# Linear attention in a vision tower: q formed with features on partitions, its row norm applied at the residual

## The chip, the cores and the metric

The kernel runs on one core of one Trainium2 chip, in fp32 throughout. The metric is the device time of one execution in microseconds (us), as the median of several runs. One further execution was taken by the hardware profiler, and all views of the profile come from that one.

## The reference

A small vision tower: a tokenizer, then two layers. Layer 0 is an attention over the four images and a mixture of six experts (top 2). Layer 1 is a linear attention and a smaller mixture of four experts with a shared branch. There are 4 images of 784 tokens of 256 features. The tokenizer puts the same tokens three times in a row, so the kernel computes one copy and writes it three times. The change concerns the linear attention of layer 1:

```python
qkv = x @ W_qkv + b_qkv                       # x: layernorm(h)
q, k, v = jnp.split(qkv, 3, axis=2)
q = q - jnp.mean(q, axis=2, keepdims=True)
k = k - jnp.mean(k, axis=2, keepdims=True)
q2, k2 = q * q, k * k
k2 = l2_normalize(k2 / (sum(k2, axis=2) + 1e-7), axis=-2)    # over the tokens
q2 = l2_normalize(q2 / (sum(q2, axis=2) + 1e-7), axis=-1)    # over the features
kv = jnp.einsum('bnc,bnd->bcd', k2, v)
attn = v + jnp.einsum('bnc,bcd->bnd', q2, kv) / math.sqrt(N)
h = h + attn @ W_out + b_out
```

Dividing q2 by its row sum and then by its row's length leaves a row divided by its length alone, apart from the small constants.

## The kernel before

The work is a sequence of stages on one core. From about 314 us on, layer 0's experts run in blocks of 256 rows. The rows of a block are loaded, transposed, taken through three matrices and written back to DRAM. For each block, `own_weights` (L1145) copies the expert's weights on DVE, `turned` (L1152) transposes on PE and copies on ACT, `hidden` (L1165) computes the two hidden layers (tile `pb`, evicted half by ACT and half by DVE into `hb`), and `rows_back` (L1184) the output (tile `pyb`, evicted by DVE into `yb`). In the loop over the later blocks (L1437) the order on DVE and SP is written out by hand: the program fixes it. The other engines' orders come from a scheduler.

In that loop, at its second block, stands the call of `centred_weights()` (L577, called at L1447). It takes the mean over the 256 output features out of the q and k weights (L580 to L582) and out of their bias (L587 to L589), all on DVE. After that, q and k come out of the matmul already centred. The bias `bqkv` lies on 112 partitions, the same row on each.

The linear attention works on *units*: each image of seven tiles of 112 tokens is cut into a unit of four tiles and one of three, eight units in all. What happens to a unit:

- `fetch` (L1360): gathers of the expert outputs, two for each tile, issued by POOL one after another. The gathers of units 0 to 2 are issued from the block loop, those of unit 2 once the last block has been written.
- `stats_one` (L1377) and `normalise` (L1395): DVE adds the gathered rows to the residual h (L1383), takes mean and variance, and makes the normalised rows `xa` (L1406).
- `x_t` (L1419): PE transposes them (helper, L297), ACT and DVE each copy one half out (L81, L83), into `lxT`.
- `q_k` (L1558): for each tile, two matmuls of 512 columns give q and k with tokens on partitions (L1574). DVE adds the bias (L1578), ACT squares each half in place and sums it along the row (L1582), and squares q2 again for the sum of its fourth powers (L1583).
- `scales` (L1591): the row factors, from those sums; ACT scales k (L1606), DVE scales q (L1607), ACT squares the scaled k (L1611). `fold` (L1614) adds these squares over the tiles on DVE (L1618 to L1623).
- `q_t` (L1625): PE transposes the scaled q (L297), ACT and DVE copy it out into `lqT`.
- `k_x` (L1630), for one image: the column norms of k2 (L1635), and the product of k2 with the normalised rows (tile `pukx`, L1648). `g_t` (L1657) and `kv_out` (L1668) make of it `kvo`, the 256 by 256 matrix that a row of q2 is multiplied with.
- `rows_out` (L1682): for two tiles at a time, one PSUM bank collects the product of `lxT` with `Wvo` (L1689) and of `lqT` with `kvo` (L1694); DVE adds it to h (L1700).

`layer1_weights` (L593) makes `Wvo`, the product of the v weights with the output weights, in unit 1's turn: PE transposes the v weights (L598), DVE copies them out as `WvT` (L602), and PE multiplies (L607).

The order around the change is set by the loop over units (from L1704), which calls these functions in a staggered way: the rows of unit u-2 are put out while unit u is begun. The scheduler moves instructions on PE, ACT and DVE from there. PSUM tiles named by `ps_tile` come from a pool of seven banks; the eighth bank, `psum_s`, serves small results in turn, among them the column norms of k2 and the gate of the last expert layer.

After the linear attention, seven groups of four tiles go through layer 1's experts (from about 666 us). They start once the h of their rows is complete.

Of the kernel before, what the change touches and what calls it, by code (L numbers as in the profile page):

```python
# [21 lines left out]
F32 = mybir.dt.float32  # L22
I32 = mybir.dt.int32
AF = mybir.ActivationFunctionType
# [3 lines left out]
P = 128  # L28
TT = 112
# [31 lines left out]
def tile_vit_tower(ctx: ExitStack, tc: tile.TileContext, a: dict, out: bass.AP):  # L61
# [10 lines left out]
    def ps_tile(name):  # L72
        return psum.tile([P, 512], F32, tag="ps", name=name)
# [251 lines left out]
    def halves(tiles):  # L325
        return [tiles[i : i + 2] for i in range(0, len(tiles), 2)]
# [3 lines left out]
    def cut(t0, n):  # L330
        return slice(t0 * TT, (t0 + n) * TT)
# [245 lines left out]
    def centred_weights():  # L577
        qkw = Wqkv[:, :, : 2 * D].rearrange("p c (i d) -> p c i d", i=2)
        mean = w1p.tile([P, 2, 2], F32, tag="mean", name="mean")
        nc.vector.tensor_reduce(mean, qkw, AX.X, ALU.add)  # L580
        nc.vector.tensor_scalar(mean, mean, 1.0 / D, None, ALU.mult)
        nc.vector.tensor_tensor(  # L582
            qkw, qkw, mean.unsqueeze(3).to_broadcast([P, 2, 2, D]), ALU.subtract
        )
        qkb = bqkv[:, : 2 * D].rearrange("p (i d) -> p i d", i=2)
        meanb = w1p.tile([TT, 2], F32, tag="meanb", name="meanb")
        nc.vector.tensor_reduce(meanb, qkb, AX.X, ALU.add)  # L587
        nc.vector.tensor_scalar(meanb, meanb, 1.0 / D, None, ALU.mult)
        nc.vector.tensor_tensor(  # L589
            qkb, qkb, meanb.unsqueeze(2).to_broadcast([TT, 2, D]), ALU.subtract  # L590
        )

    def layer1_weights():  # L593
        WvT = w1p.tile([P, 2, D], F32, tag="WvT", name="WvT")
# [742 lines left out]
    bqkv = spread(w1p, "bqkv", a["L1_attn_b_qkv"], nc.sync)  # L1337
    bout = spread(w1p, "bout", a["L1_attn_b_out"], nc.sync)

# [37 lines left out]
    def stats_one(u, j):  # L1377
        if u >= len(units) or j >= units[u][2]:
            return
        b, j0, n = units[u]  # L1380
        t = b * TPI + j0 + j
        for k in range(2):
            nc.vector.scalar_tensor_tensor(  # L1383
                h[:, t, :], ys[u][:, j, k, :], wk[:, k, t : t + 1], h[:, t, :],
                ALU.mult, ALU.add,
            )
# [166 lines left out]
    late = [early]  # L1553

    lin = linear.enter_context(tc.tile_pool(name="lin", bufs=2, reuse_waits="tile"))
    sumsof = {}

    def q_k(u, j0, j1):  # L1558

        n = units[u][2]  # L1560
        xT = xTs[u]
        if j0 == 0:
            qks[u] = lin.tile([TT, GT, 2 * D], F32, tag="qk", name="qk")
            sumsof[u] = (
                small.tile([TT, GT, 2], F32, tag="ss", name="ss"),
                small.tile([TT, GT], F32, tag="s4", name="s4"),
            )
        qk = qks[u]
        ss, s4 = sumsof[u]
        junk = lin.tile([TT, D], F32, tag="junk", name="junk", bufs=1)  # L1570
        for j in range(j0, min(j1, n)):
            pqk = ps_tile("pqk")[:TT]
            for c in range(2):
                nc.tensor.matmul(  # L1574
                    pqk, xT[:, c, cut(j, 1)], Wqkv[:, c, : 2 * D],
                    start=(c == 0), stop=(c == 1),
                )
            nc.vector.tensor_tensor(qk[:, j, :], pqk, bqkv[:, : 2 * D], ALU.add)  # L1578

            for i in range(2):  # L1580
                half = qk[:, j, i * D : (i + 1) * D]
                nc.scalar.activation(half, half, AF.Square, accum_out=ss[:, j, i : i + 1])  # L1582
            nc.scalar.activation(junk, qk[:, j, :D], AF.Square, accum_out=s4[:, j : j + 1])  # L1583
            if u:
                stats_one(u + 1, j)
        if j1 >= n and u:
            if u + 1 < len(units) and units[u + 1][2] > n:
                stats_one(u + 1, n)
            normalise(u + 1)

    def scales(u):  # L1591

        b, j0, n = units[u]
        qk = qks[u]
        ss, s4 = sumsof.pop(u)

        nc.vector.tensor_scalar(ss[:, :n], ss[:, :n], 1e-7, None, ALU.add)
        nc.scalar.activation(s4[:, :n], s4[:, :n], AF.Sqrt, bias=zero[:TT])
        nc.vector.scalar_tensor_tensor(
            ss[:, :n, 0], ss[:, :n, 0], 1e-12, s4[:, :n], ALU.mult, ALU.max  # L1600
        )
        nc.vector.reciprocal(ss[:, :n], ss[:, :n])
        uk = uks[u] = lin.tile([TT, GT, D], F32, tag="uk", name="uk", bufs=3)
        sq = lin.tile([TT, GT, D], F32, tag="sq", name="sq", bufs=1)
        for j in range(n):
            nc.scalar.activation(uk[:, j, :], qk[:, j, D:], AF.Copy, scale=ss[:, j, 1:2])  # L1606
            nc.vector.tensor_scalar(  # L1607
                qk[:, j, :D], qk[:, j, :D], ss[:, j, 0:1], None, ALU.mult
            )
        for j in range(n):  # L1610
            nc.scalar.activation(sq[:, j, :], uk[:, j, :], AF.Square)  # L1611
        return sq

    def fold(u, sq):  # L1614
# [4 lines left out]
        else:  # L1619
# [1 line left out]
            nc.vector.tensor_tensor(acc, acc, sq[:, 0:2, :], ALU.add)  # L1621
            nc.vector.tensor_tensor(acc[:, 0, :], acc[:, 0, :], sq[:, 2, :], ALU.add)
            nc.vector.tensor_tensor(acc[:, 0, :], acc[:, 0, :], acc[:, 1, :], ALU.add)  # L1623

    def q_t(u):  # L1625
        n = units[u][2]
        qT = qTs[u] = lin.tile([P, 2, GN], F32, tag="lqT", name="lqT", bufs=3)
        transposed(qks.pop(u), n, lambda c, pt: copy_out(qT[:, c, : n * TT], pt))

    def k_x(b):  # L1630

# [49 lines left out]

    def rows_out(u):  # L1682
        b, j0, n = units[u]
        xT, qT, kvo = xTs.pop(u), qTs.pop(u), kvos[b]
        for two in halves(range(n)):
            pm = ps_tile("pout")[:TT].rearrange("p (t d) -> p t d", t=2)
            for i, j in enumerate(two):
                for c in range(2):
                    nc.tensor.matmul(  # L1689
                        pm[:, i, :], xT[:, c, cut(j, 1)], Wvo[:, c, :],  # L1690
                        start=(c == 0), stop=False,
                    )
                for c in range(2):
                    nc.tensor.matmul(  # L1694
                        pm[:, i, :], qT[:, c, cut(j, 1)], kvo[:, c, :],
                        start=False, stop=(c == 1),
                    )
            t = b * TPI + j0 + two[0]
            ht = h[:, t : t + len(two), :]
            nc.vector.tensor_tensor(ht, pm[:, : len(two), :], ht, ALU.add)  # L1700

# [3 lines left out]
    for u in range(len(units) + 2):  # L1705
        b, odd = divmod(u - 2, 2)
        one_image = u >= 2 and not odd
        if u == 0:
            fetch(3)
            x_t(1)  # L1710
            q_k(0, 0, GT)
            squares[0] = scales(0)
            fold(0, squares.pop(0))
            continue
        if u < len(units):
            fetch(u + 3)
        if u == len(units):
            shared = shared1(0)
        if one_image:
            k_x(b)  # L1720
            q_t(u - 1)
        if u == 2:
            gT = g_t(0)
            kv_out(0, gT)
            rows_out(0)
            x_t(2)
        if u < len(units):
            q_k(u, 0, 2)
        if one_image and b:
            gT = g_t(b)  # L1730
        if u < len(units):
            q_k(u, 2, GT)
            if u == 1:
                lw.extend(layer1_weights())
                Wvo, bvo = lw[:2]
            squares[u] = scales(u)
        if one_image and b:
            kv_out(b, gT)
        if u == len(units) - 1:
            rows_in(0)  # L1740
            turn_rows(0)
            gate(0)
        if 2 <= u < len(units) - 1:
            x_t(u + 1)
        if u == 3:
            for k in range(3):
                residual(k)
        if u >= 2 and (b or odd):
            rows_out(u - 2)
        if u < len(units):  # L1750
            fold(u, squares.pop(u))
            if u % 2:
                q_t(u - 1)
    linear.close()

    with tc.tile_pool(name="ffn1", bufs=2) as work:
# [92 lines left out]
```

## Time and profile before

| what | us |
|---|---|
| median of 3 runs (852.16 to 854.61) | 854.3 |
| profiled execution, its own time | 813.35 |
| its span, first to last instruction | 811.6 |
| PE (TensorE matmul) busy | 735.7 |
| DVE (VectorE) busy | 514.5 |
| ACT (ScalarE) busy | 318.5 |
| block loop, the later blocks | to about 503 |
| linear attention | about 504 to 666 |
| last expert layer | about 666 to 812 |

The engines are PE, with PEld for its weight loads, DVE, ACT, POOL (GpSimd) and SP (SyncE). A line of the timeline gives the start, the duration, the engine and the line of the program, the tiles written and read, the number of instructions merged into the line, and, in brackets, the idle time before it with what ended it. An fp32 matmul leaves two records, so "x8" on PE are four matmuls. A line of the table of stages gives the stretch, its length, the busy time of each engine with its number of instructions, the granted PE clock (1.00 is full speed), the share of the DMA engines and the rate in GB/s.

### The profile page before, as it was taken

How to read it: one execution, taken by the hardware profiler on the slowest of the kernel's cores; microseconds unless marked ns; L12 is line 12 of the kernel's file. 1: busy time of each engine (PE TensorE's matmuls, PEld its weight loads, DVE VectorE, ACT ScalarE, POOL GpSimd, SP SyncE). 2: the span in 40 equal slices, each digit the busy share in tenths (PEclk: the TensorE clock that was granted, in tenths of full speed). 3: DMA queues.
4: the chain of work that ended last, by engine and by line, in shares of the span. 5: the costliest groups of instructions: out<-in, count | busy, mean ns of one | idle time of the engine just before them, and what ended most of it. 6: DMA issues, size and time to landing. Idle time of an engine off the chain costs nothing. (4 is left out here: it accounts for less than half of the span.)

```text
span 811.6 us, 11184 instructions
## 1 busy us (share of the span) xinstructions
PE 735.7 (91%) x3669; PEld 519.4 (64%) x3669; DVE 514.5 (63%) x1619; ACT 318.5 (39%) x758; POOL 132.5 (16%) x151
## 2 busy tenths in 40 slices
PE   1879998899798887999999999799999999999996
PEld 1757785555455555887888887375776675555553
DVE  3477887576668886436445756699985655554431
ACT  0414443545375475443222322627544503222221
POOL 4200000000006360760012030775000000000000
PEclk9999999999999988999999999899999999999999
DMA  8999992000001168443334234232000002333323
GB/s 182 343 426 422 420 421 85 1 0 1 0 1 56 36 207 260 137 139 104 94 101 137 92 107 131 85 86 69 1 1 1 0 20 69 88 98 93 94 85 113
DMA packets 59182, 97.52 MB, mean 120 GB/s; under 512 B 15486, under 2 KB 49460, under 8 KB 54260
## 3 DMA queue, kind: packets, MB, share of 16 engines
q1 hardware_dynamic: 52700, 81.47, 29.1%
q0 software_dynamic: 6224, 14.13, 6.1%
q10 hardware_dynamic: 200, 1.21, 0.7%
q8 instruction: 29, 0.48, 0.2%
q14 instruction: 29, 0.24, 0.1%
HBM read 31.04 MB, written 65.74 MB: 119 GB/s over the span
## 5 line engine op out<-in xcount | busy, mean ns | idle before, releaser
L901 POOL DMA_INDIRECT xrows<-xn,pos x56 | 60.2, 1074 | 274.2 <-ACT kq L665 233.4
L1369 POOL DMA_INDIRECT ys<-yrows,pos x56 | 57.0, 1018 | 142.1 <-DMA yrows<-yb 126.0
L1173 PE MATMUL pb<-xTb,own 128*128 128x256 f32 x240 | 58.8, 389 | 3.8 <-DVE r L764 1.6
L1173 PE MATMUL pb<-hb,own 128*128 128x256 f32 x240 | 57.1, 380 | 0.3 <-DVE hb L1181 0.3
L1190 PE MATMUL pyb<-own,hb 128*128 128x256 f32 x240 | 57.0, 380 | 0.2 <-ACT hb L1179 0.2
L1179 ACT ACTIVATE hb<-pb,own 128x256 f32<-128x256 f32 x74 | 35.0, 473 | 55.9 <-PE pb L1173 47.5
L297 PE MATMUL pt<-ident,xn 112*128 112x112 f32 x280 | 42.2, 282 | 12.6 <-DVE xn L482 6.9
L1173 PEld LDWEIGHTS pb<-xTb,own 128*128 128x128 f32 x240 | 44.6, 194 | 12.5 <-ACT hb L1179 1.9
L1574 PE MATMUL pqk<-Wqkv,lxT 128*112 128x512 f32 x112 | 49.7, 594 | 0.5 <-ACT lxT L81 0.5
L1190 PEld LDWEIGHTS pyb<-own,hb 128*128 128x128 f32 x240 | 45.4, 190 | 6.7 <-ACT hb L1179 0.6
L297 PEld LDWEIGHTS pt<-ident,xn 112*128 112x128 f32 x280 | 32.4, 148 | 26.6 <-ACT xn L778 9.6
L1173 PEld LDWEIGHTS pb<-hb,own 128*128 128x128 f32 x240 | 43.3, 190 | 5.9 <-DVE hb L1181 0.9
L1196 DVE TENSOR_TENSOR yb<-pyb,eb 128x512 f32<-128x512 f32 x30 | 20.7, 690 | 39.2 <-PE pyb L1190 38.8
L306 PE MATMUL pe<-xT,eW 128*128 128x448 f32 x112 | 45.2, 546 | 0.0
L1163 ACT COPY xTb<-ptb 128x512 f32<-128x512 f32 x30 | 17.5, 583 | 64.3 <-PE ptb L1159 64.3
L1181 DVE TENSOR_SCALAR hb<-pb,own 128x256 f32<-128x256 f32 x46 | 22.1, 481 | 29.5 <-PE pb L1173 29.5
L317 PE MATMUL pwo<-Wo,oT 128*112 128x256 f32 x112 | 29.0, 413 | 7.5 <-DVE oT L730 6.7
L1574 PEld LDWEIGHTS pqk<-Wqkv,lxT 128*112 128x112 f32 x112 | 19.3, 177 | 24.8 <-issue 22.7
L690 DVE SCALAR_TENSOR_TENSOR prod<-kq 128x784 f32<-128x784 f32 x32 | 30.3, 968 | 7.3 <-ACT kq L665 5.1
L1582 ACT ACTIVATE qk<-qk 112x256 f32<-112x256 f32 x56 | 22.8, 407 | 27.9 <-DVE qk L1578 25.4
L306 PEld LDWEIGHTS pe<-xT,eW 128*128 128x128 f32 x112 | 20.2, 190 | 20.9 <-issue 20.7
L1150 DVE COPY own<-ew 128x1540 f32 x30 | 28.9, 963 | 5.0 <-issue 1.5
(339 smaller groups left out, 1520.1 us busy)
## 6 DMA issues: line engine op xcount, KB each, us to landing
xrows<-nothing SPq DMA_DIRECT2D x19, 1024.0 KB
yrows<-nothing SPq DMA_DIRECT2D x19, 1024.0 KB
out_dram<-h SPq DMA_DIRECT2D x84, 112.0 KB
xb<-xrows SPq DMA_DIRECT2D x30, 256.0 KB
yrows<-yb SPq DMA_DIRECT2D x30, 256.0 KB
ew<-in_L_ffn_expert_w_dram SPq DMA_DIRECT2D x6, 768.0 KB
wb<-wd SPq DMA_DIRECT2D x28, 112.0 KB
img<-in_x_dram ACTq DMA_DIRECT2D x2, 588.0 KB
```

Source lines behind the costliest of these rows:

```text
L297: nc.tensor.transpose(pt[:, j * TT : (j + 1) * TT], xn[:, j, c * P : (c + 1) * P], ident[:TT, :TT])
L306: nc.tensor.matmul(pm[: wcols.stop - wcols.start, :n], w[:, c, wcols], xT(c), start=(c == 0), stop=(c == chunks - 1),)
L317: nc.tensor.matmul(pm[:, i, :], xT(c, t), w[:, c, :], start=(c == 0), stop=(c == chunks - 1))
L690: nc.vector.scalar_tensor_tensor(prod, qTs[s][:, o, :], 1.0, kT[:, o, t * SEQ : (t + 1) * SEQ], ALU.mult, ALU.mult, accum_out=atts[s][:, o ...
L901: put = nc.gpsimd.indirect_dma_start(out=xrows[:, :], out_offset=bass.IndirectOffsetOnAxis(ap=pos[:, k, t0 + j : t0 + j + 1], axis=0), in_ ...
L1150: nc.vector.tensor_copy(w, ewf[0][:, bass.ds(off, EW)])
L1173: nc.tensor.matmul(pm, wm[:, c, o * P : (o + 1) * P], src[:, c, :], start=(c == 0), stop=(c == 1),)
L1179: nc.scalar.activation(dst[:, o, :], pm, AF.Relu, bias=b)
L1190: nc.tensor.matmul(pm[:, t, :], src[:, c, t * P : (t + 1) * P], wm[:, c, :], start=(c == 0), stop=(c == 1),)
L1369: got = nc.gpsimd.indirect_dma_start(out=y[:, j, k, :], out_offset=None, in_=yrows[:, :], in_offset=bass.IndirectOffsetOnAxis(ap=pos[:, k, ...
L1574: nc.tensor.matmul(pqk, xT[:, c, cut(j, 1)], Wqkv[:, c, : 2 * D], start=(c == 0), stop=(c == 1),)
L1582: nc.scalar.activation(half, half, AF.Square, accum_out=ss[:, j, i : i + 1])
```

## The change

q and k are formed apart. k is formed as before, with tokens on partitions, but two tiles share a PSUM bank and one bias addition. q is formed transposed, with the weights as the stationary operand: features on partitions, up to 448 tokens in one matmul. ACT squares it at eviction and adds the bias as a column. That column, `bq`, is made in `centred_weights`, by two matmuls with a single one that turn the bias row. The transposes of q, its scaling on DVE, and the row sums of q on ACT are gone.

The row's length is taken later. ACT squares q2 once more (`q4`), matmuls with 32 columns of ones add it up over the features, ACT copies the sums to SBUF, a small matmul turns them so that tokens lie on partitions, ACT takes the root and DVE the reciprocal. `norms` does this for the unit before, between k and q of the next. `rows_out` now puts the two products into two banks; DVE adds the first to h, and then for each tile the second times the row's factor.

```diff
     def centred_weights():
...
+        pb = ps_tile("pbq")
+        for c in range(2):
+            nc.tensor.matmul(
+                pb[:, c : c + 1], bqkv[:1, c * P : (c + 1) * P], ones[:1], start=True, stop=True
+            )
+        nc.vector.tensor_copy(bq, pb[:, :2])
...
-    def q_k(u, j0, j1):
...
+    def k_of(u):
...
+        for two in halves(range(n)):
+            pk = ps_tile("pk")[:TT].rearrange("p (t d) -> p t d", t=2)[:, : len(two), :]
+            for i, j in enumerate(two):
+                for c in range(2):
+                    nc.tensor.matmul(
+                        pk[:, i, :], xT[:, c, cut(j, 1)], Wqkv[:, c, D : 2 * D],
+                        start=(c == 0), stop=(c == 1),
+                    )
+            nc.vector.tensor_tensor(
+                kr[:, two[0] : two[-1] + 1, :], pk, over(bqkv[:, D : 2 * D], len(two)), ALU.add
+            )
+            for j in two:
+                nc.scalar.activation(
+                    kr[:, j, :], kr[:, j, :], AF.Square, accum_out=ss[:, j : j + 1]
+                )
...
+    def q_of(u):
...
+        for o in range(2):
+            pq = mm_t(
+                n * TT, Wqkv, slice(o * P, (o + 1) * P), lambda c: xTs[u][:, c, : n * TT], "pq1"
+            )
+            nc.scalar.activation(qT[:, o, : n * TT], pq, AF.Square, bias=bq[:, o : o + 1])
+        nc.scalar.activation(q4[:, :, : n * TT], qT[:, :, : n * TT], AF.Square)
+
+    def norms(u):
...
+        pg = psum_s.tile([P, 512], F32, tag="pss", name="pq4")[: 32 * n, :TT]
+        for c in range(2):
+            for j in range(n):
+                nc.tensor.matmul(
+                    pg[32 * j : 32 * (j + 1), :], ones32, q4[:, c, cut(j, 1)],
+                    start=(c == 0), stop=(c == 1),
+                )
+        qn = small.tile([P, TT], F32, tag="qn", name="qn", bufs=2)[: 32 * n]
+        nc.scalar.copy(qn, pg)
+        pr = psum_s.tile([P, 512], F32, tag="pss", name="pqn")[:TT, :n]
+        nc.tensor.matmul(
+            pr, qn, ident.rearrange("p (j e) -> p j e", e=32)[: 32 * n, :n, 0],
+            start=True, stop=True,
+        )
+        r = rqs[u] = small.tile([TT, GT], F32, tag="rq", name="rq", bufs=4)
+        nc.scalar.activation(r[:, :n], pr, AF.Sqrt, bias=zero[:TT])
+        nc.vector.tensor_scalar(r[:, :n], r[:, :n], 1e-19, None, ALU.max)
+        nc.vector.reciprocal(r[:, :n], r[:, :n])
...
-    def q_t(u):
-        n = units[u][2]
-        qT = qTs[u] = lin.tile([P, 2, GN], F32, tag="lqT", name="lqT", bufs=3)
-        transposed(qks.pop(u), n, lambda c, pt: copy_out(qT[:, c, : n * TT], pt))
...
     def rows_out(u):
...
+            pm = mm_rows(two, lambda c, j: xT[:, c, cut(j, 1)], Wvo, "pxo")
+            pq = mm_rows(two, lambda c, j: qT[:, c, cut(j, 1)], kvo, "pqo")
+            nc.vector.tensor_tensor(ht, pm, ht, ALU.add)
+            for i, j in enumerate(two):
+                nc.vector.scalar_tensor_tensor(
+                    ht[:, i, :], pq[:, i, :], r[:, j : j + 1], ht[:, i, :], ALU.mult, ALU.add
+                )
...
         if u < len(units):
-            q_k(u, 0, 2)
+            k_of(u)
+            norms(u - 1)
         if one_image and b:
             gT = g_t(b)
         if u < len(units):
-            q_k(u, 2, GT)
+            q_of(u)
```

More of the change, by code (lines that the diff above doesn't have):

```diff
@@ L1338, in tile_vit_tower @@
     bout = spread(w1p, "bout", a["L1_attn_b_out"], nc.sync)
+    bq = w1p.tile([P, 2], F32, tag="bq", name="bq")
     units = [(b, j0, n) for b in range(NI) for j0, n in ((0, 4), (4, 3))]
@@ L1555, in tile_vit_tower @@
     lin = linear.enter_context(tc.tile_pool(name="lin", bufs=2, reuse_waits="tile"))
-    sumsof = {}
-    def q_k(u, j0, j1):
+    sumsof, q4s, rqs = {}, {}, {}
+    ones32 = lin.tile([P, 32], F32, tag="ones32", name="ones32", bufs=1)
+    nc.vector.memset(ones32, 1.0)
+    def k_of(u):
         n = units[u][2]
         xT = xTs[u]
[L1562 to L1566, printed above, removed]
-            )
[L1568 to L1576, printed above, removed]
-                )
[L1578 to L1586, printed above, removed]
@@ new lines, in k_of @@
+        kr = qks[u] = lin.tile([TT, GT, D], F32, tag="kr", name="kr")
+        ss = sumsof[u] = small.tile([TT, GT], F32, tag="ss", name="ss")
+        for two in halves(range(n)):
[8 more added lines that the diff above has]
+                kr[:, two[0] : two[-1] + 1, :], pk, over(bqkv[:, D : 2 * D], len(two)), ALU.add
+            )
+            for j in two:
+                nc.scalar.activation(
+                    kr[:, j, :], kr[:, j, :], AF.Square, accum_out=ss[:, j : j + 1]
+                )
+                if u:
+                    stats_one(u + 1, j)
@@ L1587, in q_k @@
+        if u:
             if u + 1 < len(units) and units[u + 1][2] > n:
@@ L1589, in q_k @@
             normalise(u + 1)
+    def q_of(u):
+        n = units[u][2]
+        qT = qTs[u] = lin.tile([P, 2, GN], F32, tag="lqT", name="lqT", bufs=4)
+        q4 = q4s[u] = lin.tile([P, 2, GN], F32, tag="q4", name="q4", bufs=1)
+        for o in range(2):
[5 more added lines that the diff above has]
+    def norms(u):
+        n = units[u][2]
+        q4 = q4s.pop(u)
+        pg = psum_s.tile([P, 512], F32, tag="pss", name="pq4")[: 32 * n, :TT]
[16 more added lines that the diff above has]
+        nc.vector.reciprocal(r[:, :n], r[:, :n])
     def scales(u):
         b, j0, n = units[u]
-        qk = qks[u]
-        ss, s4 = sumsof.pop(u)
+        kr = qks.pop(u)
+        ss = sumsof.pop(u)
         nc.vector.tensor_scalar(ss[:, :n], ss[:, :n], 1e-7, None, ALU.add)
[L1598 to L1601, printed above, removed]
         nc.vector.reciprocal(ss[:, :n], ss[:, :n])
@@ L1605, in scales @@
         for j in range(n):
[L1606 to L1609, printed above, removed]
+            nc.scalar.activation(uk[:, j, :], kr[:, j, :], AF.Copy, scale=ss[:, j : j + 1])
         for j in range(n):
@@ L1683, in rows_out @@
         b, j0, n = units[u]
-        xT, qT, kvo = xTs.pop(u), qTs.pop(u), kvos[b]
+        xT, qT, kvo, r = xTs.pop(u), qTs.pop(u), kvos[b], rqs.pop(u)
         for two in halves(range(n)):
[L1686 to L1697, printed above, removed]
             t = b * TPI + j0 + two[0]
             ht = h[:, t : t + len(two), :]
-            nc.vector.tensor_tensor(ht, pm[:, : len(two), :], ht, ALU.add)
+            pm = mm_rows(two, lambda c, j: xT[:, c, cut(j, 1)], Wvo, "pxo")
[5 more added lines that the diff above has]
+                )
     squares = {}
@@ L1710, in tile_vit_tower @@
             x_t(1)
-            q_k(0, 0, GT)
+            k_of(0)
+            q_of(0)
             squares[0] = scales(0)
@@ L1720, in tile_vit_tower @@
             k_x(b)
-            q_t(u - 1)
+        if u == len(units):
+            norms(u - 1)
         if u == 2:
@@ L1727, in tile_vit_tower @@
         if u < len(units):
-            q_k(u, 0, 2)
+            k_of(u)
+            norms(u - 1)
         if one_image and b:
@@ L1751, in tile_vit_tower @@
             fold(u, squares.pop(u))
-            if u % 2:
-                q_t(u - 1)
     linear.close()
```

## The prediction, made before the changed kernel was run

> **What bounds the kernel now.** I read the page first, then PE busy and clock by stage, then the timelines of PE and DVE at two places: where the linear attention starts, and inside the expert-block loop, where `centred_weights` is placed. The page's first line and a table of stages (us, then busy us of PE, PEld, DVE, ACT, POOL, then granted clock, DMA share, GB/s):
>
> ```profile
> PE 735.7 (91%) x3669; PEld 519.4 (64%) x3669; DVE 514.5 (63%) x1619; ACT 318.5 (39%) x758; POOL 132.5 (16%) x151
> ```
> ```profile
> 470.00:500.00 30.00, 29.37 (x149) 25.27 (x148) 19.34 (x43) 8.49 (x17) 6.22 (x6) 1.00 0.35 108
> ...
> 520.00:540.00 20.00, 16.61 (x72) 13.68 (x73) 16.98 (x55) 8.50 (x30) 15.34 (x16) 0.83 0.30 87
> 540.00:560.00 20.00, 19.52 (x72) 11.38 (x71) 19.78 (x50) 8.30 (x33) 15.73 (x15) 1.00 0.30 86
> 560.00:580.00 20.00, 20.00 (x96) 14.64 (x95) 19.69 (x56) 11.26 (x42) 1.97 (x3) 1.00 0.07 19
> ```
>
> PE is the bound in the block loop (29.4 of 30) and from 540 on. But DVE is just as full from 540 to 580 (39.5 of 40), so a new instruction pair that makes PE wait for DVE is not free there. The one large hole is at 516 to 522. PE's timeline, then DVE's:
>
> ```profile
> 515.75 0.60 PE L598 MATMUL pwv<-ident,Wqkv 128*128 128x128 f32 x4
> 522.28 3.78 PE L607 MATMUL pwvo<-Wout,WvT 128*128 128x256 f32 x8 [5.94 <-DVE WvT L602]
> ```
> ```profile
> 521.18 0.45 DVE L1383 SCALAR_TENSOR_TENSOR h<-ys,wk,h 112x256 f32<-112x256 f32 x1
> 521.55 0.67 DVE L602 COPY WvT<-pwv 128x512 f32<-128x512 f32 x1
> ```
>
> PE waits 5.94 us for a copy that stands in DVE's queue behind the additions of gathered rows (L1383). And L607 takes 3.78 us for eight records where the chain of waits has 1.72 for eight of the same size (L1689, 0.86 for four): the clock is granted at half from about 521.9 to 528.6 (0.53 over that stretch), a loss of some 3.1 us on top.
>
> Now the block loop, where the change puts two matmuls. PE, then DVE:
>
> ```profile
> 378.55 1.89 PE L1173 MATMUL pb<-hb,own 128*128 128x256 f32 x8
> 380.28 1.89 PE L1173 MATMUL pb<-xTb,own 128*128 128x256 f32 x8
> ...
> 385.53 1.13 PE L1173 MATMUL pb<-hb,own 128*128 128x256 f32 x4 [0.33 <-DVE hb L1181]
> 387.21 1.97 PE L1173 MATMUL pb<-xTb,own 128*128 128x256 f32 x8 [0.55 <-DVE own L1150]
> ```
> ```profile
> 380.48 0.48 DVE L1181 TENSOR_SCALAR hb<-pb,own 128x256 f32<-128x256 f32 x1 [0.43 <-PE pb L1173]
> 380.88 1.21 DVE L580 TENSOR_REDUCE mean<-Wqkv 128x4 f32<-128x1024 f32 x1
> ...
> 384.39 0.69 DVE L589 TENSOR_TENSOR bqkv<-bqkv,meanb 112x512 f32<-112x512 f32 x1
> 385.00 0.48 DVE L1181 TENSOR_SCALAR hb<-pb,own 128x256 f32<-128x256 f32 x1
> ```
>
> See that centring (L580 to L589) occupies DVE from 380.88 to 385.08, and that PE hardly notices: it has independent block work, and loses 0.33 and 0.55 us.
>
> [...] idle of 5.94 us, half clock for about 6.7; idle of 3.47 us before 217.43, then 0.52 over 217.43 to 221. It also shows an idle of 2.93 us (before 48.41) with the clock staying at 1.00. [...] sixteen records of L1513 (32 columns of weights) take 0.52 us in the chain.
>
> **The change part by part.** An fp32 matmul of 256 columns leaves two records and costs 0.43 us (L1689: 0.86 for four), of 512 columns 0.86 (L1574: 3.44 for eight), of 448 columns 0.755 (L306: 3.02 for eight).
>
> - *q and k.* Before, 28 tiles x 2 x 0.86 = 48.2. After, k: 56 x 0.43 = 24.1; q: per image four of 448 and four of 336 columns, 3.02 + 2.27 = 5.29, x4 = 21.1. PE: -3.0.
> - *Transposes of q* gone: 0.77 + 0.57 per image, x4: -5.4. The last 0.57 covers the wait for g, so -4.8 counts.
> - *Norms.* `ones32` matmuls like L1513: 0.52 (four tiles) and about 0.45 (three), x4 = 3.9. The turn of the norms: one matmul of three or four columns, priced by L1635 (0.34 to 0.60 for two): 0.2, x8 = 1.6. PE: +5.5.
> - *Rows out*: the same 112 matmuls, in two banks instead of one. 0 on PE. Seven banks cover it, since DVE needs 2 x 0.68 + 4 x 0.48 = 3.3 us for four tiles in which PE computes 6.9; without the cover, PE would wait at a bank.
> - *DVE* per image: q/k additions from 7 x 0.684 to 3 x 0.684 + 0.42 (-2.3), q scaling (seven of L1607, 8.4/4) -2.1, copies of qT -1.1, rows +7 x 0.46 = +3.2, small ones +0.3: -2.0. *ACT* loses the third square and its read-out (0.40 + 0.19 per tile) and gains evictions of 0.63. Neither is the bound by itself; worth 0. Two more table loads at the end (1.28 us each, as the two in that stretch) lie beside 3.0 + 6.2 us of PE work (L306, L1648): 0; if uncovered, 2.6. SP's and POOL's orders are unchanged, gathers included.
> - *New waits in the linear stage.* The turn matmul waits for ACT's copy of the norms, and in ACT's queue that copy stands behind the squares of k, which wait for DVE's addition; behind the matmul on PE stand the rest of q and all else. From DVE's place in the changed order I get waits of about 0.6, 0.6, 0.6, 0 and 1.1 us for units 3 to 7. With fewer transposes ahead of it, the column sum of k2 (L1635) now waits about 1.0 for DVE in image 1, and lxT about 1.1 in unit 3 (0.2 before). Sum +4.8. From both sides: 0 if DVE is nowhere late, 12 if each of twelve hand-overs costs 1.
> - *The WvT hole stays.* In the changed order the copy stands behind the ninth and tenth gathers (the tenth issues at 518.85, lands about 2.66 later, 521.5), then 0.45 + 0.34 + 0.13: it starts at 522.6 against 521.55. +1.0, mostly given back, as q's transposes no longer follow at half clock: 1.06 instead of 0.77 for the first eight. I count +0.7.
>
> Linear stage: -3.0 - 4.8 + 5.5 + 4.8 + 0.7 = +3.2; less the waits of before that go (0.36 + 0.68 at 536 and 537, now filled by norms of unit 1, and about 1.8 of the norms' own 5.5 that lie in that wait and in the WvT hole) = +0.4. Ends: -4 and +7.
>
> - *The bias column.* `pbq`, two matmuls of one column, reads the centred bias. In the changed order it stands on PE directly after the matmuls that began at 378.55, before those of 380.28. It can't run until L589 ends at 385.08, and PE keeps its order: the independent work of 380.28 to 385 is queued behind it. Then 0.4 for the two; 1.72 each for pb and pyb, 0.44 for ptb, 1.72 for pb: 385.5 + 5.6 = 391.1, where the next pb begins, against 387.21. By then the old waits of 0.33 and 0.55 are gone, as DVE is ahead. DVE's copy of `bq` waits for PE, and behind it hb (L1181), yb and own: all due later than PE needs them now. **+3.9**. Bounds: 3.5 to 4.2. Nothing hides it: PE is full until 500 and the gathers start only after the last block.
> - *The clock after it.* PE stands idle about 4.7 us there. After 3.47 us the trace shows 3.5 us at half, after 5.94 some 6.3: losses of 1.7 and 3.1. **+2.4**; ends 0 (as after 2.93) and 3.4.
>
> Sum: 3.9 + 2.4 + 0.4 = **+6.7**. The profiled execution of 813.35 (span 811.6) becomes 820.1. The median of the runs is 854.3, 5.0% above it; no view shows where the 41 us lie, so I carry the difference over as it is: **861.0**.
>
> **The rivals.**
> 1. *Main*: block-loop wait with half clock, linear stage even: 861.0. Chance 0.62.
> 2. *The linear stage keeps its work saving*: DVE's relief of 2.0 per image makes the new waits vanish, so -3.0 instead of +0.4: 854.3 + 6.3 - 3.0 = 857.6. For it: DVE falls from 39.5 of 40. Against it: ACT's order. 0.20.
> 3. *The hand-overs bind*: +7 instead of +0.4: 867.6. For it: DVE full at 540 to 580. Against it: 7 banks of slack. 0.12.
> 4. *Not slower: the WvT hole closes.* If the copy comes early, 5.94 of idle and 3.1 of half clock go: 6.3 + 0.4 - 9.1 = -2.4, 851.9. [...] Against it: two gathers ahead of it that land at 520.3 and 521.5. 0.06.
>
> That the change does not do what it says is excluded by the changed order: no transposes of q remain.
>
> **The numbers.** A measurement here tells about 0.3% (2.6 us) from no change. Faster (under 851.7): half of case 4, 0.03. Same: the other half and the low tail of case 2, 0.09. Slower: 0.88. Range 856.5 to 867.0: it leaves out case 4, the low tail of 2 and the upper half of 3, some 0.16.
>
> **What would show it.** PE waiting about 4.8 us for DVE's bqkv at the `pbq` line near 380, then matmuls of twice the length for 3 to 7 us, and the last block about 6 us later. The WvT wait still there, its copy 1 us later against the gathers. Waits of up to 1 us on the turn matmul for ACT's copy. From the first gather to the end of the linear stage: as long as before within 3 us. I am wrong if PE passes `pbq` without a wait, if the WvT wait shrinks below 2 us, or if that last stretch changes by over 4 us.

## The result and the profile after

The changed kernel takes 861.62 us (median of 4 runs, 859.44 to 863.78), the kernel before 853.23 (4 runs, 850.7 to 854.61) beside it: ratio 1.0102, 95% interval 1.0063 to 1.014. That is +8.4 us, where +6.7 and 861.0 were forecast. The sum was met, with some luck: the interval is 5.4 to 11.9 us. Of its three terms one was right, one too small, and one, if near, near only by accident, as the rest shows.

One fact is needed to read the numbers. The runs came on several chips: the kernel before takes about 850 us on some of them (medians 849.0 and 851.3 on two, 844 to 857 in 52 runs) and 813 to 815 on others (813.2 and 815.1 on two, 809 to 818 in 66 runs, but for one slow run of 834). The profile before (813.35 us) looks like the second kind, the times beside it (852 to 854) like the first; I call them *850 chips* and *813 chips*. Ratios below are always of runs on one chip.

The profiled execution after took 860.77 us (span 859.1). Its first line, and the same table of stages (us, then busy us of PE, PEld, DVE, ACT, POOL, then granted clock, DMA share, GB/s):

```profile
PE 745.6 (87%) x3809; PEld 537.3 (63%) x3809; DVE 505.9 (59%) x1603; ACT 313.3 (36%) x678; POOL 129.9 (15%) x151
```
```profile
470.00:500.00 30.00, 30.00 (x155) 26.12 (x154) 19.84 (x40) 10.19 (x19) 0.00 (x0) 1.00 0.31 99
530.00:550.00 20.00, 9.09 (x41) 5.42 (x39) 8.13 (x23) 6.57 (x20) 15.12 (x17) 0.76 0.31 90
550.00:570.00 20.00, 1.49 (x6) 1.09 (x6) 0.71 (x3) 1.77 (x5) 10.44 (x12) 0.50 0.25 72
570.00:590.00 20.00, 18.35 (x78) 14.79 (x79) 14.82 (x51) 5.22 (x15) 8.22 (x8) 0.80 0.16 47
```

The block loop is as full as before. The new thing is 530 to 570: 40 us in which PE works 10.6, DVE 8.8 and ACT 8.3, while POOL goes on (25.6). No engine there is a bound; all wait. The end of that stretch on PE, then on ACT, with the idle time before each row and what ended it:

```profile
551.09 0.53 PE L1626 MATMUL pqn<-ident,qn 128*112 128x4 f32 x2 [9.83 <-issue]
551.48 1.09 PE L604 MATMUL pwv<-ident,Wqkv 128*128 128x128 f32 x4
570.11 3.78 PE L613 MATMUL pwvo<-Wout,WvT 128*128 128x256 f32 x8 [17.53 <-DVE WvT L608]
```
```profile
550.78 0.25 ACT L1624 COPY qn<-pq 128x112 f32<-128x112 f32 x1 [9.88 <-remote]
560.59 0.54 ACT L1608 ACTIVATE lqT<-pq,bq 128x336 f32<-128x336 f32 x1 [9.55 <-issue]
568.99 0.27 ACT L1631 ACTIVATE rq<-pqn,zero 112x4 f32<-112x4 f32 x1 [7.86 <-remote]
```

Three evictions of PE's results on ACT start 8 to 10 us apart, although the matmuls they read are shown as done (those of the q that `lqT` reads end by 541.25 in the trace, 19 us before the read). "remote" says that the profile finds no instruction that had just ended and so released the wait; "issue" says that it shows no event just before the start. For the first and the third of these reads the trace has the semaphore events at 550.76 and 568.97, while the matmuls are shown as done by 537.10 and 551.62. Between the first two POOL issues a gather every 1.23 us. This could be read as the price of the new chain of norms (qn, pqn, rq). The first experiment tests that.

The other place, in the block loop, on PE:

```profile
388.11 1.89 PE L1179 MATMUL pb<-hb,own 128*128 128x256 f32 x8
394.69 1.01 PE L594 MATMUL pbq<-ones,bqkv 1*128 1x1 f32 x4 [4.69 <-DVE bqkv L589]
395.63 3.78 PE L1179 MATMUL pb<-xTb,own 128*128 128x256 f32 x8
399.20 2.56 PE L1196 MATMUL pyb<-own,hb 128*128 128x256 f32 x8
401.60 0.60 PE L1165 MATMUL ptb<-ident,xb 128*128 128x128 f32 x4
```
```profile
380.00:394.69 14.69, 10.00 (x52) 8.39 (x50) 9.22 (x14) 2.80 (x6) 0.00 (x0) 0.97 0.23 75
394.69:401.50 6.81, 6.81 (x20) 5.72 (x21) 0.64 (x2) 0.48 (x1) 0.00 (x0) 0.57 0.00 0
401.50:420.00 18.50, 18.50 (x96) 16.08 (x95) 9.14 (x14) 5.20 (x10) 0.00 (x0) 1.00 0.27 86
```

This is what was forecast: PE waits 4.69 us for the centred bias, and eight records of pb then take 3.78 us instead of 1.89. The granted clock is 0.57 over the 6.8 us that follow the wait. Cut where it changes, the same stretch shows that the half clock began 0.97 us before PE could go on:

```profile
390.00:393.71 3.71, 0.00 (x0) 0.00 (x0) 3.60 (x5) 0.00 (x0) 0.00 (x0) 1.00 0.32 97
393.72:394.69 0.97, 0.00 (x1) 0.00 (x1) 0.86 (x2) 0.00 (x0) 0.00 (x0) 0.50 0.00 0
394.69:400.54 5.85, 5.85 (x16) 4.86 (x17) 0.64 (x2) 0.48 (x1) 0.00 (x0) 0.50 0.00 0
400.56:402.00 1.44, 1.44 (x10) 1.26 (x9) 0.20 (x1) 0.00 (x0) 0.00 (x0) 1.00 0.00 0
```

### The profile page after: what moved, and what is told of

It is laid out like the page before. It is cut to its first block, busy times and chain, and to the rows that moved or that the text cites. A ratio compares the mean times of both kernels' runs of the same rounds, so it can differ in the third digit from the quotient of the medians.

```text
span 859.1 us, 11378 instructions
## 1 busy us (share of the span) xinstructions
PE 745.6 (87%) x3809; PEld 537.3 (63%) x3809; DVE 505.9 (59%) x1603; ACT 313.3 (36%) x678; POOL 129.9 (15%) x151
## 4 chain that ended last, share of the span: by engine, by line
PE 69%; DVE 14%; ACT 5%; issue 4%; DMA 4%; another core or an unknown queue 2%; SPq 1%; POOL 0%; DVEq 0%; ACTq 0%; POOLq 0%
PE pb L1179 12%; PE pyb L1196 6%; PE pkv L306 5%; PE pe L306 5%; PE ps L306 4%; PE pukx L1679 3%; PE pqo L317 3%; PE pxo L317 3%; PE ps L1832 3%; PE pt L297 3%; PE pq L306 3%; PE pk L1581 2%; PE pw L317 2%; DVE st L470 2%
## 5 line engine op out<-in xcount | busy, mean ns | idle before, releaser
L1380 POOL DMA_INDIRECT ys<-yrows,pos x56 | 55.0, 981 | 176.0 <-DMA yrows<-yb 142.6
L1179 PE MATMUL pb<-xTb,own 128*128 128x256 f32 x240 | 64.2, 415 | 12.9 <-issue 5.4
L1179 PEld LDWEIGHTS pb<-xTb,own 128*128 128x128 f32 x240 | 47.8, 208 | 23.3 <-issue 7.2
L1169 ACT COPY xTb<-ptb 128x512 f32<-128x512 f32 x30 | 17.5, 585 | 74.0 <-PE ptb L1165 58.8
L317 PEld LDWEIGHTS pwo<-Wo,oT 128*112 128x112 f32 x112 | 21.4, 197 | 15.3 <-DVE oT L736 8.7
L317 PE MATMUL pwp<-Wp,xTln_g 128*112 128x256 f32 x112 | 28.3, 410 | 2.3 <-ACT xTln_g L492 2.3
L1394 DVE SCALAR_TENSOR_TENSOR h<-ys,wk,h 112x256 f32<-112x256 f32 x56 | 26.0, 475 | 7.0 <-DMA ys<-yrows,pos 6.8
```

The lines of the kernel that those rows point to most:

```text
L317: nc.tensor.matmul(pm[:, i, :], xT(c, t), w[:, c, :], start=(c == 0), stop=(c == chunks - 1))
L1179: nc.tensor.matmul(pm, wm[:, c, o * P : (o + 1) * P], src[:, c, :], start=(c == 0), stop=(c == 1),)
L1380: got = nc.gpsimd.indirect_dma_start(out=y[:, j, k, :], out_offset=None, in_=yrows[:, :], in_offset=bass.IndirectOffsetOnAxis(ap=pos[:, k, ...
L1394: nc.vector.scalar_tensor_tensor(h[:, t, :], ys[u][:, j, k, :], wk[:, k, t : t + 1], h[:, t, :], ALU.mult, ALU.add,)
```

## The experiments

For each I give the ratio to the kernel before on the same chip and, from the timeline of its one profiled execution, two lengths: the *block loop* (start of the first to start of the last pb matmul) and the *linear stage* (start of the first pk or pqk matmul to the end of the last pout or pqo). Where the chip is left blank it is not on record with the run. The kernels called *late column* have the column of the second experiment, and the edit named after it.

| kernel | chip | ratio (95% interval) | block loop | linear stage |
|---|---|---|---|---|
| before, first profile | | | 180.4 | 162.2 |
| before again | 850 | | 194.7 | 183.3 |
| column only | 850 | 1.0128 (1.0083 to 1.0173) | 200.1 | 183.0 |
| column only, again | 850 | 1.0117 (1.0075 to 1.0159) | 201.8 | 186.7 |
| after | | 1.0102 (1.0063 to 1.014) | 203.2 | 188.1 |
| after, again | 850 | 1.0121 (1.0076 to 1.0166) | 201.8 | 191.8 |
| late column | 850 | 1.0064 (1.004 to 1.0088) | 193.8 | 187.1 |
| late column, two ys | 813 | 0.9974 (0.9955 to 0.9992) | 181.2 | 159.9 |
| late column, two ys, again | 850 | 0.9997 (0.9976 to 1.0017) | 195.6 | 183.7 |
| before, two ys | 813 | 0.999 (0.9968 to 1.0012) | 180.4 | 162.1 |
| late column, spaced | 813 | 1.0213 (1.0181 to 1.0245) | 198.3 | 159.6 |
| late column, early WvT | 813 | 1.0034 (1.0017 to 1.0052) | 181.1 | 163.7 |
| late column, early WvT, again | 850 | 1.0097 (1.0064 to 1.0131) | 193.6 | 192.3 |
| late column, one ys | 813 | 1.0012 (0.999 to 1.0033) | 181.4 | 162.7 |

**Before again.** No edit.

> The kernel before, unchanged, profiled once more. Theory A (the 41 us between the first profile of before, 813.35, and its timed runs, 853.2, are stalls of ACT, PE and DVE of several us each, like those that the profile of after shows at 342, 541 to 569): this profile shows 850 to 856 us, and a handful of waits of 5 to 10 us put down to issue or remote. Theory B (the stalls belong to the changed kernel): 812 to 816 us again, no such waits.

849.38 us, span 847.7, as theory A has it. The late waits are in the kernel before too. ACT, then PE:

```profile
538.37 0.20 ACT L1582 ACTIVATION_READ_ACCUMULATOR qk<-qk 112x1 f32 x1
544.69 0.42 ACT L1583 ACTIVATE junk<-qk 112x256 f32<-112x256 f32 x1 [6.12 <-remote]
550.29 0.30 ACT L1598 ACTIVATE s<-s,zero 112x3 f32<-112x3 f32 x1 [4.90 <-remote]
561.59 0.53 ACT L81 COPY lqT<-pt 128x448 f32<-128x448 f32 x1 [10.47 <-remote]
```
```profile
536.84 3.78 PE L607 MATMUL pwvo<-Wout,WvT 128*128 128x256 f32 x8 [5.51 <-issue]
562.67 5.48 PE L1648 MATMUL pukx<-xa,uk 112*128 112x258 f32 x16 [17.75 <-ACT uk L1606]
```

So the holes after are not the change's own. Nor do only PE's results come late. L1583 reads what ACT itself wrote in L1582, done by 538.57, and L1598 reads the sums that L1583 left by 545.20; in the trace both waits end with an event of ACT's own semaphore, 6.1 and 4.9 us after ACT's last work. Only the third, for `pt`, is for PE. The two profiles of *column only* below, with the same linear stage, show the same.

The holes also place what "no view shows" in the prediction: against the first profile the span is 36.1 us longer; the block loop takes 14.3 of it (10.6 where the scatters overlap its start, 3.8 where the eight gathers of unit 0 run out), the linear stage 21.1, together 35.4. These lie beside or right behind POOL's indirect transfers.

**Late column.** The two pbq matmuls and the copy move two blocks later:

```
+
+    def bias_column():
         pb = ps_tile("pbq")
         for c in range(2):
...
             if i == NEARLY + 1:
                 centred_weights()
+            if i == NEARLY + 3:
+                bias_column()
```

> The changed kernel, with the two matmuls of the bias column and the copy of it moved two blocks later in the block loop, when the centred bias has long been written. Theory of the prediction (the wait at pbq costs 3.9 and the half clock after it 2.4): 6.3 us less than the changed kernel's 861.6, 855.3, that is 2 us above before or equal to it. Rival (the new hand-overs of the linear stage carry the loss, the wait at pbq is absorbed): 860 to 862, as the changed kernel.

PE now passes without waiting:

```profile
402.17 0.60 PE L596 MATMUL pbq<-ones,bqkv 1*128 1x1 f32 x4
402.70 1.99 PE L1181 MATMUL pb<-xTb,own 128*128 128x256 f32 x8
```

The column costs 0.7 us in this place: I compare the start of each pb matmul with that of the same matmul in *before again*, and the difference steps by 0.7 at the column. The time of 855.65 us is the expected one, but the kernel before takes 848.98 on this chip: 6.7 us more than before, and not 0 to 2. The ratio falls from 1.0102 (1.0121 when measured again) to 1.0064, some 3 to 5 us, on other chips; 6.3 is not excluded, as the intervals are 2 to 4 us to either side. The WvT wait (16.1) and a 12.8 us wait for pqn stay.

**Column only.** The kernel before, with the lines of the diff in `centred_weights` and the tile `bq`, and nothing else.

> The kernel before with the bias column alone added in centred_weights; nobody reads it. Theory of the prediction: 6.3 us more than before, 859.5 (5.6 to 7.3 more). Rival (the linear stage carries the loss): within 2 us of before.

> The kernel before with the bias column alone, formed in centred_weights. My recorded steps give 3.9 for the wait and 2.4 for the clock: +6.3 us, whatever the chip (the place lies outside the gathers). Against it, theory K: the first measurement of this kernel, 10 us, was no accident, the column costs 10; or 3 us, as the change with and without it had.

+10.4 and +9.3 us by medians (859.38 against 848.98; 860.59 against 851.29), where 6.3 was expected. The wait is the same, 4.69:

```profile
393.38 1.01 PE L594 MATMUL pbq<-ones,bqkv 1*128 1x1 f32 x4 [4.69 <-DVE bqkv L589]
```

Compared pb by pb with *before again*, four traces have nearly the same step at this place and none gives it back in the blocks that follow: 7.3 and 7.0 (column only), 6.9 and 7.0 (after). Both intervals reach down to it (7.0 to 14.7 us, and 6.4 to 13.5). Where the 2 to 3 us lie that the medians show beyond it, the profiles can't tell: the first is an execution of 851.67, 7.7 us below its kernel's median; the repeat has 3.4 more in the linear stage, 186.7 against 183.3. That part is open.

**Two ys buffers** (`ys` holds the gathered rows of a unit), which make POOL wait for DVE's additions between units (13.07 us after the 22nd gather, on the 850 chip below):

```
-        y = ys[u] = lina.tile([TT, GT, 2, D], F32, tag="ys", name="ys", bufs=3)
+        y = ys[u] = lina.tile([TT, GT, 2, D], F32, tag="ys", name="ys", bufs=2)
```

> The changed kernel with its late column, and the gathered rows (ys) in two buffers instead of three, so that GpSimd has to wait for VectorE's additions between units and can't issue 28 gathers in one go of 34 us. Theory S (TensorE's signals to ScalarE come 5 to 10 us late as long as gathers are issued every 1.23 us): of the three waits of ScalarE near 540 to 560 (11.2, 10.3, 5.8 us with three buffers) at most one stays, the stretch from the first k matmul to the last of the rows out falls from 187 us to about 170, and the time from about 855 to 838 to 845. Rival I (the gathers have nothing to do with those waits): the three waits stay, the time is 855 within 2 us, or later by what the delayed rows cost.

> The kernel before with ys in two buffers. Theory S: its waits of 6.1, 4.9 and 10.5 us of ScalarE and the 17.8 us of TensorE for uk go or shrink below 3 us, the linear stage falls from 183 us to about 166, the time from 849 to 830 to 838. Rival I: 849 within 2 us, or slower. For the difference of the two kernels: if the changed kernel pays more only because its chain of norms meets more of the late signals (theory C), the late-column kernel and this one end within 2 us of each other in the linear stage; if its extra is its own work and its own waits (theory H), it stays 4 to 6 us longer.

Both ran on a chip that takes 813.2 for the kernel before, and there nothing comes late (ACT's waits put down to remote or issue are under 0.8 us from 500 to 620), so neither theory was tried. They answer another question: what the linear stage costs without the late waits. It is 159.9 us against 162.1, the change's work *saves* 2.2. On PE, with waits:

```profile
512.94 0.59 PE L1623 MATMUL pq<-q,ones 128*32 128x112 f32 x16 [2.37 <-ACT q L1613]
517.48 0.36 PE L1630 MATMUL pqn<-ident,qn 128*112 128x4 f32 x2 [1.49 <-ACT qn L1628]
521.52 3.67 PE L615 MATMUL pwvo<-Wout,WvT 128*128 128x256 f32 x8 [3.19 <-DVE WvT L610]
```

The norms of unit 0 wait 2.37 and 1.49; PE thus reaches pwvo later, and waits there 3.19 instead of 5.94.

On an 850 chip:

> The late-column kernel with two ys buffers. On a chip where the kernel before takes 813: 0.997 of it, as measured. On one where it takes 850: theory S (late signals only while gathers are issued back to back; here GpSimd must wait between units) gives a linear stage below 175 us and a time 8 to 15 us under the kernel before's; rival I gives 187 us and 1.006.

Here the theory met its case. POOL's run, which is 28 gathers with three buffers, ends after 22 (523.36 to 549.23), and PE's full work resumes at 555.41, 32.1 us after the run began. With three buffers it takes 40.4 (late column), 40.5 and 40.4 (the two of after). The difference of 8.4 compares with 6 gathers x 1.23 = 7.4. But the stage came to 183.7 and not "below 175", and the ratio to 0.9997, not to 8 to 15 us less. The direction of theory S holds, its size does not: two of ACT's three late waits were still there. Rival I (187 us and 1.006) fails as well: the ratio's interval, 0.9976 to 1.0017, lies below that of the three buffers, 1.004 to 1.0088, though on another chip.

```profile
546.13 0.53 PE L1630 MATMUL pqn<-ident,qn 128*112 128x4 f32 x2 [11.21 <-issue]
555.41 3.75 PE L615 MATMUL pwvo<-Wout,WvT 128*128 128x256 f32 x8 [7.80 <-DVE WvT L610]
```

**Spaced gathers.** Memsets of a scratch tile after each gather of units 3 to 7:

```
                 tc.add_to_no_dep_group("fetched", got.ins)
+                if u >= 3:
+                    for _ in range(6):
+                        nc.gpsimd.memset(pause, 0.0)
```

> The late-column kernel with three ys buffers, and about 2 us of memsets of a scratch tile on GpSimd after every gather of units 3 to 7, so that gathers are 3 us apart instead of 1.23. Theory S: the late signals become rarer and shorter (waits of ScalarE on TensorE's signals under 3 us each instead of 11.2, 10.3 and 5.8), linear stage 168 to 178 us instead of 187. Theory S2 (what delays is GpSimd being busy at all, whatever it does): the waits stay or grow. Rival I: the waits stay at 10 us, time 855 or more.

It tested something else. The memsets wait for nothing and were placed early in POOL's queue, between the scatters: POOL is busy 75.0 of the 90 us from 330 to 420, PE waits 12.8 us for a load of rows there, and the gathers still come every 1.23 us. The block loop is 17 us longer (830.89 us). The linear stage, on an 813 chip and with three ys buffers, is 159.6: the gain above does not depend on the number of buffers.

**Early WvT.** `layer1_weights` is called in the first unit, ahead of the additions of units 2 and later (and one unit less has its residual added afterwards):

```
         if u == 0:
...
             q_of(0)
+            lw.extend(layer1_weights())
+            Wvo, bvo = lw[:2]
...
-            if u == 1:
-                lw.extend(layer1_weights())
-                Wvo, bvo = lw[:2]
```

> The late-column kernel with Wv.Wo formed in the first unit, before the gathers of units 2 and later are added, so that the WvT copy no longer stands on VectorE behind the norms' rq. If each hand-over from TensorE to ScalarE in the gathers' stretch pays its own delay (theory C), the WvT wait of 16.1 us falls below 3, the chain loses what stood behind it, and the time falls by 8 to 15 us, to 840 to 847. If all hand-overs there simply last until the run of gathers has ended (theory E: the end of the gathers sets the end of the stretch), the wait moves to another instruction and the time stays within 3 us of 855.

> The late-column kernel with Wv.Wo formed in the first unit. On a chip where the kernel before takes 813: 1.003 of it, as measured. On one where it takes 850: theory E (the late signals last until the run of gathers has ended, and what counts is how much TensorE has done by then) gives the 5.3 us of Wv.Wo and bvo back: linear stage 180 to 183 us instead of 187, ratio 0.999 to 1.003. Theory C (each hand-over pays by itself): 172 to 178 us.

Slower on both kinds: linear stage 163.7 and 192.3. On the 813 chip PE still waits for WvT (4.2). On the 850 chip that wait became small (4.3), and the hole moved to the next hand-over (PE's waits: us in total, times, longest us):

```profile
PE pqn L1630 <- ACT qn L1628: 25.5, 2, 23.1
PE pwvo L615 <- issue: 4.3, 1, 4.3
```

PE resumes at 563.69, 39.7 us after POOL's run began, as without the edit. So removing one wait gains nothing in this stretch; theory C falls. Theory E has the moment of resumption right, but its 180 to 183 us did not come: the work done ahead was not given back, and the edit costs some 4 us on the 813 chip as well (163.7 against 159.6 and 159.9), which was not traced to a cause.

**One ys buffer**, with each unit's gathers called for after the additions of the unit before:

```
-        y = ys[u] = lina.tile([TT, GT, 2, D], F32, tag="ys", name="ys", bufs=3)
+        y = ys[u] = lina.tile([TT, GT, 2, D], F32, tag="ys", name="ys", bufs=1)
...
         if u == 0:
-            fetch(3)
...
-        if u < len(units):
-            fetch(u + 3)
...
             k_of(u)
+            fetch(u + 2)
             norms(u - 1)
```

> The late-column kernel with one ys buffer, a unit's gathers being asked for only when the additions of the unit before have been issued: runs of at most 8 gathers (10 us) with a pause after each, in place of one run of 28 (34 us). Theory E (TensorE's signals come late until some 6 us after the last gather of a run, so the length of the run of gathers sets when full work starts again; runs ended at 549 to 563 so far and TensorE resumed at 555 to 570): on a chip that takes about 850 for the kernel before, TensorE resumes before 545, the linear stage falls from 187 us to 165 to 175, ratio 0.975 to 0.990. On a chip that takes 813: 0.997 if the rows are still in time, up to 1.005 if each unit waits for them. Rival L (signals are late beside any gathers, also short runs, and what one hold loses is lost at the next): linear stage 183 us or more, ratio 1.00 or above.

It met an 813 chip (815.06 for the kernel before) and shows only its price there: runs of at most 8 gathers, linear stage 162.7, ratio 1.0012. Whether short runs remove the late waits was not settled.

**After again.**

> The changed kernel as it is, beside the kernel before on the same chip. If this chip runs the kernel before at about 813 us (no late signals in the gathers' stretch), the linear stage should be 2 us shorter than before's 162 (as the late-column kernel had 160) and the column cost 6 us in the block loop: ratio 1.004 to 1.006. If it runs it at about 850 (late signals), the linear stage should be 4 to 5 us longer than before's and the ratio 1.009 to 1.014.

An 850 chip: 862.03 us against 851.29, +10.7. Beside column only on the same chip (860.59) the rest of the change is worth +1.4 by medians, within the scatter of either. The late waits are as in the first profile: WvT 16.8, pqn 12.1. The changed kernel itself was not run on an 813 chip; from the parts (late column -2.1 by the ratio 0.9974, its column 0.7 less, the early one 7.0 more) I would expect about +4 there, an estimate.

## Why the prediction was right, and where it was not

- **The bias column, +3.9: right.** The order on PE, the wait (4.7 forecast, 4.69 measured), the place and the fact that nothing gives it back are as predicted. The pb matmuls behind pbq did stay behind it: their operands were written by 388.95 (`xTb`, ACT) and 389.60 (`own`, DVE), and they began at 395.63, after pbq. The whole step of 6.9 to 7.3, less the clock's part below, leaves 4.0 in each of the four traces (3.5 to 4.2 was the range).
- **The clock after it, +2.4: too small.** I took 4.8 us at half rate, between two rows of before. In all four traces with the early column the clock stood at half for 6.83 us, of which 0.3 to 1.0 lay in the wait. PE worked 5.9 to 6.6 us at half, a loss of 2.9 to 3.3, inside the range that I gave (0 to 3.4). The 5.94 us hole of before reads the same: half from 521.33 to 528.16 (I had 521.9 to 528.6), PE at work from 522.28, a loss of 2.9. The step differs from trace to trace (6.9 to 7.3) by as much as the part of the 6.83 us that fell into the wait. There was nothing between the two rows to take: of the half-clock stretches in the profiles of before and after that begin by 800 us, one lasts 30.7 us (the late stretch of after, from 543.9) and all others 3.41 or 6.83. And the length of the wait does not tell which: the wait of 3.47 us is followed by 3.41 at half before (217.54 to 220.95) and by 6.83 after (212.81 to 219.64). So the estimate should have been one of the two, less the part in the wait; it came to the longer.
- **The linear stage, +0.4: the working was wrong, however near the number.** On 813 chips the stage is 2.2 us *shorter*, which is rival 2 (-3.0). The step that failed is "New waits in the linear stage ... Sum +4.8". The stage before (first profile), then with late column and two ys:

```profile
503.73:665.88 162.15, 154.05 (x664) 106.59 (x663) 122.95 (x367) 76.28 (x276) 42.31 (x42) 0.98 0.12 33
501.35:661.24 159.89, 151.28 (x800) 116.71 (x799) 115.21 (x355) 66.70 (x191) 43.74 (x42) 0.99 0.12 34
```

PE's idle time rose by 0.5 in all, 8.1 to 8.6; its busy time fell by 2.8, of which 1.2 is the shorter half clock of the next point. After pwvo PE waits for lxT 0.7, gT 0.7 and rq 0.2, in all 1.6 (before: gT 1.3, lxT 0.5, g 0.4, in all 2.2). There is no wait on the turn matmul of units 3 to 7 and none on pn; DVE, relieved by 5.4 us of busy time between 500 and 668 (125.92 to 120.50), is nowhere late. The only such waits are in unit 0 (2.37 and 1.49), ahead of the WvT hole, which is 2.75 shorter for them.

- **The WvT hole, +0.7: the copy right, the hole wrong.** Measured from the first gather of the run, the copy starts at 14.8 us instead of 13.8: the +1.0 forecast. But PE arrives later, so the wait is 3.19, and PE works 3.4 us at half instead of 5.9 (3.8 in the spaced run): a loss of 1.7 instead of 2.9. From the first k matmul to pwvo the change costs 1.6, after it gains 3.9.
- **"Carry the difference over as it is": wrong in substance.** The 41 us are in the main waits that end late, and the change meets them differently. On 850 chips the profiles of the changed linear stage are 187.1 to 191.8, those with before's linear stage 183.0 to 186.7. My own sign of being wrong, the stretch from the first gather to the end of the linear stage, changed by +6.0 (438.7 to 713.3 against 433.4 to 702.0), so it was met: the reasoning was wrong there, though the total was not. By what the medians add up to it is +1.4 (after again less column only), or +6.0 (the late column, less its own 0.7). These don't agree to better than 5 us, and the part of the linear stage in the +8.4 stays open between about 1 and 6. That the total came out near the forecast is luck in this part: the 41 us are not a constant that both kernels carry.
- **Rival 4** (hole closes) is out: the wait is 17.5 and 16.8 us after, and still 3.2 on the 813 chip. **Rival 3** (hand-overs bind, +7) has the right size for some 850 traces but the wrong cause: on the 813 chips it is absent, and there DVE is nowhere late. What comes with it on the 850 chips is waits that end late.

What orders the late stretch is shown only in part. In all eight traces with the late waits PE's full work resumes 6.2 to 7.2 us after the last gather of POOL's long run starts (555.86 to 562.67, 562.87 to 570.11, and so on), whatever instruction waits there, and in the one trace with a shorter run that moment comes earlier. I read this as one and the same moment in before and after, with the difference in how much PE has done by then; what sets the moment was not shown. Before, pwvo and pbvo (some 5 us: 536.84 to 542.32 in *before again*) are done ahead of it; after, the chain of norms stands ahead of them and they come behind it. From resumption to the end of the stage it is 138.4 to 142.2 us in the three traces with before's linear stage, 142.9 to 147.2 in the three with the changed one and three ys buffers. That fits, but the early-WvT kernel, which did the product ahead, had 148.7 left; so the account is not complete.

A version that clearly beats both was not found. The late column with two ys buffers is 0.26% faster than the kernel before on an 813 chip (0.9974, 0.9955 to 0.9992) and equal on an 850 chip (0.9997).

## What to carry to other kernels

Two matmuls of one column cost 7 us where PE had to wait in order for DVE, and 0.7 two blocks later: before adding a tiny instruction to an engine that is full, look at when its operand is ready and what stands behind it, and count the half clock by the stretches that the trace shows (3.41 or 6.83 us here), less what lies in the wait. When the profiled execution and the median differ by 5%, find where before forecasting: a second profile of the unchanged kernel put 35 of 36 us beside the indirect transfers. And where waits lie in a row, removing one may show only the next (with the early WvT, 4.3 us were left of that wait and 23.1 stood at the next); read what ends the last.

## What was not expected of the hardware

In the traces of 850 us, while POOL issues gathers or scatters in a row (one per 1.23 us), waits end late: ACT's in the linear stage that are put down to remote or issue last 4.9 to 11.2 us. In those of 813 us, with the same program and the same rate of gathers, every wait of ACT that is put down to these is under 0.8 us, from 500 to 620. What is late are not PE's results alone. With before's linear stage, two of ACT's long waits are for its own work (*before again*: work over by 538.57, event at 544.66), so there the signal is late, by 6.1 us in this case. For PE's results it can't be told whether the matmul or its signal is late, as matmul ends are modelled. A hand-over from DVE to ACT in the same stretch of *after* was prompt: an addition of k that ends at 539.54 is followed by its square at 539.58. The gathers keep their pace and their packets their duration (one per 1.23 us, and 4 KB in 0.269 us on average in *before* and 0.268 in *after*), so the transfers are not slower. Why chips differ is open.
